# One transposition per head in the 256-key blocks, and the last group's queries transposed straight from the projection's pairs

## The chip, the core and the metric

The kernel runs on one core of a Trainium2 chip. The metric is device time in microseconds (us), the median of three runs; lower is better. The engines by their names in the profile: PE is TensorE (PEld its weight loads), DVE is VectorE, ACT is ScalarE, POOL is GpSimd, SP is SyncE, which computes nothing and issues DMAs (a line with SPq is one such issue).

## The reference

`x` is [1024, 512]. It is normalized by rows, goes through causal attention and through a feed-forward block whose weights are 4-bit integers, and the second gates the first:

```python
def attn(x, Wq, Wk, Wv, Wo, q_norm_w, k_norm_w):   # 32 heads, 8 groups of keys and values, head 128
    q, k, v = (x @ Wq.T), (x @ Wk.T), (x @ Wv.T)   # split into heads
    q, k = rmsnorm(q, q_norm_w), rmsnorm(k, k_norm_w)
    scores = einsum('bkgqd,bksd->bkgqs', qg, k) / sqrt(128)
    bias = where(rel > 0, -1e30, slopes * rel)     # causal, with a slope per head
    out = einsum('bkgqs,bksd->bkgqd', softmax(scores + bias), v)
    return out @ Wo.T

xn = layernorm(x)
s = attn(xn)
g = silu((silu(xn @ gate) * (xn @ up)) @ down)     # gate, up, down: (int - zero) * scale, 1792 wide
return x + s * g
```

## The kernel before

**Precision.** Every product is made in 16-bit halves. A float32 operand is split into a high half and a low half in fp16, and a product is three matmuls (high x high, high x low, low x high; `mm3`, L107 to L111). So "a split" is a copy to the high half (mostly on ScalarE) and a subtraction for the low half (on VectorE or GpSimd). The two halves lie side by side in one tile, so that one DMA can transpose both.

**Phases.** The feed-forward block comes first (0 to about 218 us). Then come twelve projections (to about 491 us): for each pair of groups one of keys and values (`kv`) and two of queries (`q`), each of eight tiles of 128 rows. The steps of attention start inside the last two projections, one at every second tile, and fill the rest of the time.

**A projection** (`class Projection`, from L484). `norms` (L509) sums the squares of the raw weights over the partitions by a matmul with ones; its PSUM tile comes from `spare` (L481). `tile` (L560) makes one row tile by 12 matmuls into a PSUM bank; banks come in turn from the tags "m" and "o", with two buffers each, and ScalarE copies the result into `f` and sums the squares of each head. After each four tiles `queue_half` (L754) sets due steps for what follows: `inverse` and `newton` (the inverse root), `normalize` on GpSimd (L622, L626), `halves` on VectorE (L628: a copy and a subtraction, giving the pair `a16`), `transposed` (L642: a DMA transposition of the pair into `tr`, L644) and `store` (L647: `tr` to DRAM). The last projection, that of group 7's queries, is treated apart: its eight tiles are spread over the attention steps, one pair of tiles in each fourth block. `wo_factors` (L794) prepares a scale for each group's rows of the output weight, with one matmul of its own (L801).

**Attention.** Work is cut into units (group, block of 256 queries, head), four units to a block, and each unit into two query tiles of 128 rows; one query tile is one step. A block of queries `qb` looks at the first (qb+1) x 256 keys, so the blocks are named by their keys here: 256, 512, 768 or 1024. The order of the blocks in a group is `FIRST_ORDER` for group 0 (1024, 768, 512, 256), `ORDER` for groups 1 to 6 (768, 1024, 256, 512) and `LAST_ORDER` for group 7 (768, 1024, 512, 256) (L45 to L47). `step(n)` (L960) is a software pipeline written out by hand. In step n:

- `scores` (L834) for query tile n, in PSUM tag "s" of two 2-bank buffers;
- `exponentials` (L845) for tile n-1: VectorE adds the bias and takes the row's minimum (L854, in the profile DVE row and pf), ScalarE makes the exponentials and their sum (L855);
- `split_hi` (L858) for n-3, on ScalarE (L865), and `split_lo` (L867) for n-4, on VectorE (L874), which ends with the DMA transposition of the probabilities, `pT<-p` (L875), issued by SP;
- `values` (L879) for n-9 (`AV_LAG`): the matmuls `av` of the transposed probabilities with the values;
- `heads_hi` and `heads_lo` for n-10, which split the heads' outputs, and `out_proj` (L910) and `accumulate` (L935) for the block before.

```python
        for stage, lag in ((exponentials, 1), (split_hi, NQT + 1), (split_lo, NQT + 2)):
            if at(n - lag):
                stage(*at(n - lag))
```

In the 256-key block the first query tile has 128 keys, the second 256: their pairs of halves are 256 and 512 columns wide (2 and 4 column blocks of 128).

**What else a step carries.** In the second head of a block SP loads the next block's queries from DRAM (`load_queries`, L788, `qT<-qd`). In the fourth head of the third block of a group `relative` (L822; `trel`, 1024 columns, on GpSimd, L830) and `load_keys` for the next group are done, and in the fourth head of the fourth block `load_values`. The output weight's rows are loaded, scaled (L813) and split (L819, L820, the tile `wol`) by `load_wo`, `scale_wo` and `split_wo` over eight steps in each group. In group 7 `gate_load` fetches the gate and x for each block, 1 MB each.

**Queues.** All DMAs are issued by SP, in the order of the program, and an issue that waits holds back those behind it. The same holds for each engine's instructions. The program's order is the order in which the functions above are called.

Of the kernel before, what the change touches and what calls it, by code (L numbers as in the profile page):

```python
# [21 lines left out]
P = 128  # L22
# [3 lines left out]
HKV = 8  # L26
# [18 lines left out]
FIRST_ORDER = (3, 2, 1, 0)  # L45
ORDER = (2, 3, 0, 1)
LAST_ORDER = (2, 3, 1, 0)  # L47
# [3 lines left out]
FINISH_BLOCK = 3  # L51
KEYS_BLOCK = 2
VALUES_BLOCK = 3
# [5 lines left out]
GATE_LOADS = [25, 26, 28, 30]  # L59
GATE_SUMS = [27, 28, 30, 31]  # L60
GATE_STEP = 2
PF_BUFS = 5
P16_BUFS = 5

# [7 lines left out]
def attention_gated_by_ffn_kernel(ctx, tc, x, gu_w, gu_z, gu_s, dn_w, dn_z, dn_s, wq, wkv, wo, qnw, knw, out):  # L72
# [408 lines left out]
    def spare(k, name):  # L481
        return ps2(name)[:, 0, :] if k else pair(name)[:, 0, :]

    class Projection:  # L484
# [24 lines left out]
        def norms(self):  # L509

            n = self.n
            pn = spare(self.k, f"n2_ps{self.k}")
            te.matmul(pn[:, 256 : 256 + n], lhsT=ones_bf, rhs=self.sb[:, :n], start=True, stop=True)
            if self.kind == "kv":
                for j in range(KT):
                    te.matmul(pn[:, :256], lhsT=ones_bf, rhs=self.sq[:, j, :], start=j == 0, stop=j == KT - 1)
            self.am = wp.tile([P, NH], F32, tag="am", name=f"am_{self.name}", bufs=2)[:, :n]
            ve.tensor_scalar(self.am, pn[:, 256 : 256 + n], 1.0 / W_SCALE**2, 1e-30, ALU.mult, ALU.max)
            rsqrt_seed(self.am, self.am)
            self.eps = eps[:, self.k, :n]  # L520
            ve.scalar_tensor_tensor(self.eps, self.am, 1e-6 * X_SCALE**2, self.am, ALU.mult, ALU.mult)
            if self.kind == "q":
                ve.tensor_tensor(self.eps, self.eps, steep, ALU.mult)
            if self.kind == "kv":
                self.al = wp.tile([P, 256], F32, tag="al", name=f"al{self.i}")
                ve.tensor_scalar(self.al, pn[:, :256], DM * (X_SCALE / V_SCALE) ** 2, 1e-30, ALU.mult, ALU.max)
                rsqrt_seed(self.al, self.al)
# [100 lines left out]
        def halves(self, t):  # L628
            f = self.f[t // HT][:, t % HT]
            n = self.n  # L630
            if self.kind == "q":
                a16 = fq.tile([P, 2, n, HD], F16, tag="a16", name=f"q16_{self.i}_{t}", bufs=5)
                hi, lo = a16[:, 0], a16[:, 1]
            else:
                a16 = fq.tile([P, 2, 2, HD], F16, tag="a16", name=f"k16_{self.i}_{t}", bufs=5)
                hi, lo = a16[:, :, 0, :], a16[:, :, 1, :]
                ve.tensor_tensor(f, f, wn.unsqueeze(1).to_broadcast([P, 2, HD]), ALU.mult)
            ve.tensor_copy(hi, f)
            ve.tensor_tensor(lo, f, hi, ALU.subtract)
            defer(2 if self.k == len(projections) - 1 else 1, lambda: self.transposed(t, a16))  # L640

        def transposed(self, t, a16):  # L642
            tr = fq.tile([P, 2 * self.n, P], F16, tag="tr", name=f"tr_{self.name}_{t}", bufs=5)
            sp.dma_start_transpose(tr, a16.rearrange("p a g d -> p (a g d)"))  # L644
            defer(4 if self.k == len(projections) - 1 else 2, lambda: self.store(t, tr))
# [108 lines left out]
    def queue_half(p, half):  # L754

        last = p is projections[-1]

        def due(steps, i, f):
            t = half * HT + i
            c = TILES - early + BS * (NB * (1 + t // 2) + FINISH_BLOCK) + 4 * (t % 2) if last else clock[0] + i  # L760
            finishing.setdefault(c + steps, []).append(f)

        due(0, 0, lambda: p.inverse(half))
        if p.by_root:
            due(1, 0, lambda: p.newton(half, True))
        else:
            for i in range(3):
                due((i + 1) // 2, 0, lambda i=i: p.newton(half, i == 0))
        for i in range(HT):
            t = half * HT + i  # L770
            due(4, i, lambda t=t: p.halves(t))
            due(2, i, lambda t=t: p.normalize(t))

    NB = S // QB
    blocks = [(g, qb) for g in range(HKV) for qb in (FIRST_ORDER if g == 0 else ORDER if g < HKV - 1 else LAST_ORDER)]
    units = [(g, qb, hh) for g, qb in blocks for hh in range(NH)]
# [11 lines left out]
    def load_queries(g, qb):  # L788
        qT[g, qb] = ap1.tile([P, NQT, 2, NH, P], F16, tag="qT", name=f"qT{g}_{qb}")
        sp.dma_start(  # L790
            qT[g, qb].rearrange("p t a g q -> p t (a g q)"), qd[g][qb * NQT : (qb + 1) * NQT].rearrange("t p c -> p t c")
        )

    def wo_factors(k):  # L794

        if k == 0:
            ve.tensor_tensor(rvs, rv, rv, ALU.mult)
            ve.tensor_tensor(swo16, rvs, swo, ALU.mult)
        elif k == 1:
            wo_ps.append(ps2("wo_ps")[:, 0, :HKV])  # L800
            te.matmul(wo_ps[0], lhsT=ones_bf, rhs=swo16, start=True, stop=True)  # L801
        else:
            ve.tensor_scalar(sg, wo_ps.pop(), 1.0 / W_SCALE**2, 1e-30, ALU.mult, ALU.max)
            rsqrt_seed(sg, sg)
            ve.reciprocal(isg, sg)
            ve.tensor_tensor(rvs, rv, sg, ALU.mult)
# [51 lines left out]
    def split_hi(u, qt):  # L858
# [5 lines left out]
        p16[u, qt] = ap1.tile([P, NT, 2, P], F16, tag="p16", name=f"p16_{u}_{qt}", bufs=P16_BUFS)[:, :nk]  # L864
        se.activation(p16[u, qt][:, :, 0, :], pf[u, qt], AF.Copy, scale=scale[:, qt : qt + 1])  # L865

    def split_lo(u, qt):  # L867
# [6 lines left out]
        ve.scalar_tensor_tensor(lo, p, scale, hi, ALU.mult, ALU.subtract)  # L874
        sp.dma_start_transpose(  # L875
# [22 lines left out]
    def heads_hi(u):  # L898
        oh = late[0].tile([P, QB], F16, tag="oh", name=f"oh{u}", bufs=8)
        ol = late[0].tile([P, QB], F16, tag="ol", name=f"ol{u}", bufs=8)  # L900
        se.activation(oh, av_ps[u], AF.Copy, scale=1.0 / P_SCALE)  # L901
        oT[u] = (oh, ol)

    def heads_lo(u):
        oh, ol = oT[u]
        ve.scalar_tensor_tensor(ol, av_ps.pop(u), 1.0 / P_SCALE, oh, ALU.mult, ALU.subtract)

    nb = len(units) // NH

    def out_proj(b, i, part):  # L910
        if part == 0:
            op_ps[b, i] = last_ps[i] if b == nb - 1 else ps1("m", f"op{b}_{i}")
        oh, ol = oT[b * NH + part]
        g = blocks[b][0]
        cols = slice(i * P, i * P + P)
        mm3(op_ps[b, i], (oh[:, cols], ol[:, cols]), (woh[g, part], wol[g, part]), part == 0, part == NH - 1)
# [3 lines left out]
    def gate_load(b):  # L920
        g, qb = blocks[b]
# [4 lines left out]
        gates[b] = gx  # L926

    def gate_partial(b, i):

        g, qb = blocks[b]  # L930
        gx, yt = gates[b], y_[0][:, qb * NQT + i, :]
# [3 lines left out]
    def accumulate(b, i):  # L935
        g, qb = blocks[b]
        ps = op_ps.pop((b, i))
# [7 lines left out]
        else:  # L945
            gt = gates[b][:, 0, i]
            ve.scalar_tensor_tensor(gt, ps, undo, gt, ALU.mult, ALU.mult)
            (ge if (b, i) == (nb - 2, NQT - 1) else ve).tensor_tensor(gt, gt, yt, ALU.add)
# [3 lines left out]
    nn, BS = len(order), NH * NQT  # L952
    late, y_ = [], []
# [6 lines left out]
    def step(n):  # L960
        nonlocal last_ps
        if n < nn:
            u, qt = order[n]
            g, qb, hh = units[u]
            b = u // NH
            if qt == 0 and hh == 1 and b + 1 < nb:
                load_queries(*blocks[b + 1])
            if qt == 0 and hh == 3 and g + 1 < HKV:
                if b % NB == KEYS_BLOCK:
                    relative(g + 1)  # L970
                    load_keys(g + 1)
                elif b % NB == VALUES_BLOCK:
# [11 lines left out]
        b, r = divmod(n - AV_LAG - BS - 2, BS)  # L984
        if 0 <= b < nb - 1 and r % NH == NH - 1 and n < nn + AV_LAG + 1:
            accumulate(b, r // NH)
        finish_step()
        m = n - AV_LAG - BS - 1

        def project():  # L990
            b, r = divmod(m, BS)
            if 0 <= b < nb - 1:
                out_proj(b, *divmod(r, NH))
# [5 lines left out]
        if done is not None and done // NH == nb - 1:  # L999
            if done % NH == 0:  # L1000
                last_ps = [ps2(f"op_last{i}")[:, 0, :] for i in range(NQT)]
            for i in range(NQT):
                out_proj(nb - 1, i, done % NH)
            if done % NH == NH - 1:
                accumulate(nb - 2, NQT - 1)
                for i in range(NQT):
                    accumulate(nb - 1, i)
        b, r = divmod(n - AV_LAG, BS)
        if r == 2 and b in GATE_LOADS:
            gate_load(nb - NB + GATE_LOADS.index(b))  # L1010
        if b in GATE_SUMS and 0 <= r - GATE_STEP < NQT:
            gate_partial(nb - NB + GATE_SUMS.index(b), r - GATE_STEP)
        for lead, act in ((WO_SPLIT, split_wo), (WO_SCALE, scale_wo), (WO_LOAD, load_wo)):
            w, r = divmod(m + lead, NB * BS)
            if 0 <= w < HKV and r in range(0, 2 * NH, 2):
                act(w, r // 2)

    last_ps, wo_ps = None, []
    relative(0)
    last_kv = len(projections) - 3  # L1020
    WO_FACTORS = [(last_kv, 5), (last_kv, 7), (last_kv + 1, 0)]
    early = 0
    for k, p in enumerate(projections):
        if k == len(projections) - 3:
            load_keys(0)
            load_values(0)
            load_queries(*blocks[0])
        for t in range(NT):
# [7 lines left out]
            if (k, t) in WO_FACTORS:  # L1036
                wo_factors(WO_FACTORS.index((k, t)))
            p.tile(t)
            finish_step()
            if t % HT == HT - 1:  # L1040
                queue_half(p, t // HT)
# [49 lines left out]
```

## Time and profile before

| | |
|---|---|
| median of three runs | 1071.33 us (1070.93 to 1071.74) |
| the profiled execution | 1077.16 us, span 1075.4 us |
| busy, share of the span | PE 94%, PEld 55%, DVE 82%, ACT 75%, POOL 38% |
| DMA queue of SP | 450,014 packets, 205.3 MB, 86.0% of 16 engines' time |
| idle of PE before `av`, for `pT<-p` | 26.1 us |
| idle of ACT before the high halves (L865), for `pT<-p` | 25.3 us |

The page cuts the span into 40 slices of 26.9 us each. A digit is the busy share of an engine in tenths, in the row PEclk the clock that TensorE was granted in tenths of full speed, and in the row DMA the mean busy share of the core's 16 DMA engines. Slices 0 to 7 are the feed-forward block, 8 to 17 the projections, and attention runs from slice 18 on. An idle time is put down to what ended it ("<- DMA pT<-p": the landing of a transposed tile of probabilities).

### The profile page before, as it was taken

The page shows a single profiled execution, that of the slowest core. Times are in us where ns is not written, and L with a number is a line of the kernel's source. Part 1 is how long each engine was busy: PE and PEld are TensorE (multiplying, and loading weights), DVE is VectorE, ACT ScalarE, POOL GpSimd, SP SyncE. Part 2 cuts the span into 40 slices and gives each one's busy share as a digit, 9 for nine tenths or more (in the row PEclk, how much of TensorE's full clock was granted, in tenths as well). Part 3 has the DMA queues.
Part 4 walks back from the last instruction along what each step waited for, and adds up shares of the span by engine and source line. Part 5 has one row for each costly group of instructions (what it writes and reads, how often), then busy time and mean ns, then how long its engine had stood idle before and what let it go on. Part 6 is the DMA issues. An engine that isn't in the chain of part 4 may idle for free.

```text
span 1075.4 us, 18459 instructions
## 1 busy us (share of the span) xinstructions
PE 1012.7 (94%) x5913; PEld 588.1 (55%) x5913; DVE 884.4 (82%) x1745; ACT 803.0 (75%) x2160; POOL 409.0 (38%) x375
## 2 busy tenths in 40 slices
PE   7899899999999999898899999999999899999996
PEld 4444377844444444345556566566565566665663
DVE  7888996638778787787789899798998797979985
ACT  5777645878778687688779688786896787978872
POOL 1688753124536446361404306016033050150542
PEclk8999999999999999999999999999999999999998
DMA  5133269446989989999989999899998999999995
GB/s 200 32 115 109 79 172 300 159 138 164 224 229 183 239 205 254 257 174 222 213 172 214 185 221 218 181 230 186 205 213 184 188 210 185 209 237 208 239 202 127
DMA packets 450111, 206.49 MB, mean 192 GB/s; under 512 B 394530, under 2 KB 404062, under 8 KB 450014
## 3 DMA queue, kind: packets, MB, share of 16 engines
q1 hardware_dynamic: 450014, 205.32, 86.0%
q8 instruction: 46, 0.75, 0.3%
q14 instruction: 51, 0.42, 0.1%
HBM read 79.42 MB, written 29.36 MB: 101 GB/s over the span
## 4 chain that ended last, share of the span: by engine, by line
PE 50%; DVE 13%; ACT 13%; DMA 12%; issue 8%; POOL 2%; SPq 1%; DVEq 0%; ACTq 0%; POOLq 0%
DMA pT<-p 7%; PE gu_ps L262 6%; PE av L109 3%; PE s L109 3%; PE s L111 3%; PE s L110 3%; PE av L111 3%; PE av L110 3%; PE op L111 3%; PE op L110 3%; PE op L109 3%; ACT pf L855 3%; ACT p L865 3%; DVE pf L854 2%; PE ps_q L109 2%
## 5 line engine op out<-in xcount | busy, mean ns | idle before, releaser
L874 DVE SCALAR_TENSOR_TENSOR p<-pf,row,p 128x1024 f16<-128x1024 f32 (+7 forms) x256 | 221.1, 864 | 36.1 <-ACT p L865 33.4
L855 ACT ACTIVATE pf<-pf,row 128x1024 f32<-128x1024 f32 (+7 forms) x256 | 197.3, 771 | 46.7 <-DVE row L854 44.2
L854 DVE CUSTOM_DVE_ANT_0 pf<-s,trel,cs 128x1024 f32<-128x1024 f32 (+7 forms) x256 | 207.3, 810 | 16.7 <-PE s L111 15.5
L865 ACT ACTIVATE p<-pf,row 128x1024 f16<-128x1024 f32 (+7 forms) x256 | 196.7, 769 | 29.5 <-DMA pT<-p 25.3
L109 PE MATMUL av<-pT,vT 128*128 128x256 f16 (+1 forms) x640 | 169.4, 265 | 26.3 <-DMA pT<-p 26.1
L813 POOL TENSOR_SCALAR wor<-wor,rvs 128x512 f32<-128x512 f32 x32 | 53.0, 1656 | 313.0 <-DMA wor<-in_wo 313.0
L110 PE MATMUL av<-pT,vT 128*128 128x256 f16 (+1 forms) x640 | 169.4, 265 | 0.0
L111 PE MATMUL av<-pT,vT 128*128 128x256 f16 (+1 forms) x640 | 169.2, 265 | 0.0
L109 PE MATMUL s<-kT,qT 128*128 128x512 f16 (+3 forms) x384 | 126.1, 328 | 4.2 <-DVE row L854 4.1
L110 PE MATMUL s<-kT,qT 128*128 128x512 f16 (+3 forms) x384 | 126.2, 329 | 0.0
L111 PE MATMUL s<-kT,qT 128*128 128x512 f16 (+3 forms) x384 | 124.6, 328 | 0.0
L109 PEld LDWEIGHTS <-vT 128*128 128x128 f16 x640 | 63.2, 99 | 71.5 <-issue 17.3
L109 PE MATMUL ps_q<-wh_q,xth 128*128 128x512 f16 x256 | 97.8, 382 | 0.3 <-ACT wh_q L551 0.3
L110 PE MATMUL ps_q<-wl_q,xth 128*128 128x512 f16 x256 | 97.7, 381 | 0.4 <-DVE wl_q L552 0.4
L111 PE MATMUL ps_q<-wh_q,xtl 128*128 128x512 f16 x256 | 97.5, 381 | 0.0
L110 PE MATMUL op<-wol,oh 128*128 128x512 f16 x248 | 94.5, 381 | 1.0 <-POOL wol L820 1.0
L111 PE MATMUL op<-woh,ol 128*128 128x512 f16 x248 | 94.7, 382 | 0.0
L109 PE MATMUL op<-woh,oh 128*128 128x512 f16 x248 | 94.4, 381 | 0.0
L110 PEld LDWEIGHTS <-vT 128*128 128x128 f16 x640 | 63.2, 99 | 40.6 <-issue 2.7
L901 ACT ACTIVATE oh<-av 128x256 f16<-128x256 f32 x128 | 47.9, 374 | 42.8 <-PE av L111 41.6
L626 POOL TENSOR_TENSOR f_q<-f_q,inv_q 128x512 f32<-128x512 f32 x64 | 77.0, 1229 | 1.3
L820 POOL TENSOR_TENSOR wol<-wor,woh 128x512 f16<-128x512 f32 x32 | 50.2, 1570 | 66.4 <-ACT woh L819 66.4
(193 smaller groups left out, 2267.8 us busy)
## 6 DMA issues: line engine op xcount, KB each, us to landing
qd<-tr_q SPq DMA_DIRECT2D x64, 256.0 KB, 3.7
qT<-qd SPq DMA_DIRECT2D x32, 512.0 KB, 4.5
wq<-in_wq SPq DMA_DIRECT2D x32, 256.0 KB, 4.0
wo_sq<-in_wo SPq DMA_DIRECT2D x8, 1024.0 KB, 9.0
wor<-in_wo SPq DMA_DIRECT2D x32, 256.0 KB, 3.6
gui<-in_gu_w SPq DMA_DIRECT2D x13, 512.0 KB, 3.7
wkv<-in_wkv SPq DMA_DIRECT2D x16, 256.0 KB, 3.8
vd<-v SPq DMA_DIRECT2D x8, 512.0 KB, 4.3
```

The source lines that it names most:

```text
L109: te.matmul(ps, lhsT=lh, rhs=rh, start=first, stop=False)
L110: te.matmul(ps, lhsT=lh, rhs=rl, start=False, stop=False)
L111: te.matmul(ps, lhsT=ll, rhs=rh, start=False, stop=last)
L262: te.matmul(banks[j][:, k, :], lhsT=w[:, j, ws], rhs=x[:, j, k * 512 : k * 512 + 512], start=x is xth, stop=x is xtl)
L626: ge.tensor_tensor(f, f, ib, ALU.mult)
L813: ge.tensor_scalar(wor[g, i], wor[g, i], rvs[:, g : g + 1], None, ALU.mult)
L820: ge.tensor_tensor(wol[g, i], raw, woh[g, i], ALU.subtract)
L854: ve.tensor_tensor_reduce(p, ps, trel[g][:, S - w :], cs[:, hh : hh + 1], 3e38, ALU.add, ALU.min, least[:, c])
L855: se.activation(p, p, AF.Exp, bias=least[:, c], scale=-1.0, accum_out=total[:, c])
L865: se.activation(p16[u, qt][:, :, 0, :], pf[u, qt], AF.Copy, scale=scale[:, qt : qt + 1])
L874: ve.scalar_tensor_tensor(lo, p, scale, hi, ALU.mult, ALU.subtract)
L901: se.activation(oh, av_ps[u], AF.Copy, scale=1.0 / P_SCALE)
```

## The change

1. In the 256-key blocks both query tiles of a head share one tile of pairs, laid out as (key tile, half, query tile, key). The quarter that the mask leaves out, the second key tile of the first query tile, is set to zero by GpSimd. One DMA transposition of eight column blocks per head takes the place of one of two and one of four; it is issued after the second tile's low half.
2. The last projection's pairs are kept, in five buffers, and each is transposed straight into the queries' tile `qT` of group 7, at a fixed step (`LAST_QUERIES`). The transposition into `tr`, the store to DRAM and the load from it fall away for this group. The steps of the pairs are given one by one (`LAST_PAIRS`), as are those of the inverse roots (`LAST_ROOTS`). The last projection makes its rows 512 to 1023 first.
3. `relative` and `load_keys` go from step 22 of a group to step 4 of it, `load_values` from step 30 to step 24.
4. `norms` takes its PSUM tile from tag "m" in place of "s". The matmul of `wo_factors` joins that of the last projection's `norms`, in the same tile.
5. The schedule is written as tables (`q_at`, `op_at`, `acc_at`, `GATE_LOADS`, `GATE_SUMS`) that name the same steps as before for `load_queries`, `out_proj`, `accumulate` and the gate.

```diff
+KEYS_STEP = 4
+VALUES_STEP = 24
+LAST_ROOTS = {1: 24, 0: 36}
+LAST_PAIRS = {4: 46, 5: 78, 6: 110, 7: 142, 2: 174, 3: 221, 0: 224, 1: 229}
+LAST_QUERIES = {4: 217, 5: 219, 6: 225, 7: 227, 2: 233, 3: 235, 0: 241, 1: 243}
...
     def spare(k, name):
-        return ps2(name)[:, 0, :] if k else pair(name)[:, 0, :]
+        return ps1("m", name) if k else pair(name)[:, 0, :]
...
+            wo = pn[:, 384 : 384 + HKV]
+            if self.k == len(projections) - 1:
+                te.matmul(wo, lhsT=ones_bf, rhs=swo16, start=True, stop=True)
...
+            if self.k == len(projections) - 1:
+                wo_factors(wo)
...
-            defer(2 if self.k == len(projections) - 1 else 1, lambda: self.transposed(t, a16))
+            if self.k == len(projections) - 1:
+                last_pairs[t] = a16
+            else:
+                defer(1, lambda: self.transposed(t, a16))
...
         def due(steps, i, f):
-            t = half * HT + i
-            c = TILES - early + BS * (NB * (1 + t // 2) + FINISH_BLOCK) + 4 * (t % 2) if last else clock[0] + i
+            if last and i is None:
+                c = TILES + LAST_ROOTS[half]
+            elif last:
+                c = TILES + LAST_PAIRS[half * HT + i] - 4
+            else:
+                c = clock[0] + (i or 0)
             finishing.setdefault(c + steps, []).append(f)
...
+    def last_queries(t):
+        g, qb = HKV - 1, t // NQT
+        if (g, qb) not in qT:
+            qT[g, qb] = ap1.tile([P, NQT, 2, NH, P], F16, tag="qT", name=f"qT{g}_{qb}", bufs=2)
+        sp.dma_start_transpose(
+            qT[g, qb][:, t % NQT].rearrange("p a g q -> p (a g) q"), last_pairs.pop(t).rearrange("p a g d -> p (a g d)")
+        )
...
-        p16[u, qt] = ap1.tile([P, NT, 2, P], F16, tag="p16", name=f"p16_{u}_{qt}", bufs=P16_BUFS)[:, :nk]
+        if units[u][1]:
+            p16[u, qt] = ap1.tile([P, NT, 2, P], F16, tag="p16", name=f"p16_{u}_{qt}", bufs=P16_BUFS)[:, :nk]
+        elif qt == 0:
+
+            both = ap1.tile([P, NT, 2, P], F16, tag="p16", name=f"p16_{u}", bufs=P16_BUFS)
+            both = both.rearrange("p t a k -> p (t a k)")[:, : 4 * NQT * P].rearrange("p (t a i k) -> p t a i k", t=2, a=2, i=NQT)
+            ge.memset(both[:, 1, :, 0, :], 0.0)
+            for i in range(NQT):
+                p16[u, i] = both[:, : i + 1, :, i, :]
+            p16[u] = both
...
+        if u in p16:
+            if qt == NQT - 1:
+                sp.dma_start_transpose(
+                    pT[u][:, :NQT].rearrange("p t a (i q) -> p (t a i) q", i=NQT),
+                    p16.pop(u).rearrange("p t a i k -> p (t a i k)"),
+                )
+            return
...
-                if b % NB == KEYS_BLOCK:
+                if n % (NB * BS) == KEYS_STEP:
                     relative(g + 1)
                     load_keys(g + 1)
-                elif b % NB == VALUES_BLOCK:
+                elif n % (NB * BS) == VALUES_STEP:
                     load_values(g + 1)
...
-            if (k, t) in WO_FACTORS:
-                wo_factors(WO_FACTORS.index((k, t)))
-            p.tile(t)
+            if (k, t) == (len(projections) - 3, HT + 1):
+                wo_squares_sums()
+
+            row = t if k < len(projections) - 1 else (t + HT) % NT
+            p.tile(row)
             finish_step()
             if t % HT == HT - 1:
-                queue_half(p, t // HT)
+                queue_half(p, row // HT)
```

## The prediction

> **What bounds the kernel now.** I read, in this order: the page's slices, what TensorE waited for, the DMA queue's timeline, TensorE's timeline at one wait, and windows cut at the blocks. The profiled execution took 1077.16 us with a span of 1075.4; the median of the runs shown is 1071.33, so the sums below are made against 1077.16 and scaled by 1071.33 / 1077.16 = 0.9946.
>
> ```profile
> PE   7899899999999999898899999999999899999996
> PEclk8999999999999999999999999999999999999998
> DMA  5133269446989989999989999899998999999995
> ```
> TensorE is the bound from end to end (94% busy), and from slice 18 on, where attention runs, the DMA engines are as full. What TensorE still loses there stands in its list of waits (us in total, times, longest):
>
> ```profile
> PE av L109 <- DMA pT<-p: 26.1, 21, 3.2
> PE s L109 <- DVE row L854: 4.1, 6, 1.7
> PE wo_ps L801 <- DVE swo L798: 2.6, 1, 2.6
> ```
> So 26 us go to probabilities that are not yet transposed. Why they are late is seen in SP's queue, here over the blocks of 256 and 512 keys of group 4:
>
> ```profile
> 818.98 2.14 SPq L875 DMA_TRANSPOSE pT<-p  x1
> 821.17 1.30 SPq L644 DMA_TRANSPOSE tr_q<-q  x1
> 822.57 3.83 SPq L875 DMA_TRANSPOSE pT<-p  x3
> 826.49 0.53 SPq L790 DMA_DIRECT2D qT<-qd  x1
> 827.12 1.17 SPq L875 DMA_TRANSPOSE pT<-p  x1
> 828.38 0.53 SPq L649 DMA_DIRECT2D qd<-tr_q  x1
> 828.97 1.24 SPq L644 DMA_TRANSPOSE tr_q<-q  x1
> 830.25 5.00 SPq L875 DMA_TRANSPOSE pT<-p  x3
> ```
> Start and length: one issue follows the other without a gap. By the view of line 875 an issue lasts at least 1167 ns however small the tile (median 1428, 3813 at most). VectorE had finished a low half at 838.77 that SP issued only at 844.62, 5.9 us late. SP is the bound of these two blocks. In the blocks of 768 keys the same lateness is back to 0.03 us, in those of 1024 it grows to 2 or 3 us, because there the DMA engines are full (share 1.14).
>
> A wait of over 2 us costs twice (start, length of one, idle before it):
>
> ```profile
> 843.86 0.28 PE L109 MATMUL av<-pT,vT 128*128 128x256 f16 x1 [2.18 <-DMA pT<-p]
> 845.68 0.63 PE L109 MATMUL s<-kT,qT 128*128 128x512 f16 x1
> 848.42 0.38 PE L111 MATMUL op<-woh,ol 128*128 128x512 f16 x1
> ```
> The 512-column matmul goes from 0.38 to 0.63 us for about 3.4 us, and the window over 836.4 to 858.1 has a granted clock of 0.92 of 1.00: (1 - 0.92) x 21.7 = 1.7 us lost again. [...]
>
> **The change, part by part.**
>
> 1. *One transposition per head in the 256-key blocks.* It removes 32 issues of 1.17 to 1.24 us (two of 2 and 4 column blocks become one of 8). An 8-block transposition has rows: the queries' and those of 512 keys, 1.23 to 1.25 us when SP is not held back. SP saves about 8 x 1.2 - 4 x 1.25 = 4.6 us per group, in the block where it falls behind. The queries of the last group also leave groups 1 to 4: two issues of 1.3 and two of 0.53 us each, 3.7 us per group. The lateness at the end of a 1024-key block (2 to 3 us) is then gone within the next block, and the 512-key block after it (8 x 1.25 + 0.56 us of queries, about 11.5 us with the gaps) fits its 13 to 14 us. So the waits for tiles of 256 and 512 keys go. Counting the av matmuls (values run 9 steps behind scores), they are, from group 1 to the start of group 7: 0.56, 0.75, 0.35, 1.41, 1.91, 0.30, 2.18, 2.29, together 9.75 us, and 1.7 us of half clock. Six waits end with a 1024-key tile and stay: 1.36, 2.30, 0.97, 1.25, 0.26, 1.59. Six in group 0 stay (6.5 us). The last, 2.15 at 1055.2, is the first tile of the last block behind 1 MB of gate loads; one issue less brings it forward by 1.2 us, its doubled size takes back some 0.6: -0.7 (between 0 and -3.9 with the half clock after it).
> 2. *The queries' way, middle groups.* TensorE's waits of 0.88 (593), 1.01 (742, for POOL's wol) and 1.07 (744) stand next to that projection's small POOL and VectorE steps, which move away: -2.1, taking the two larger.
> 3. *What lands elsewhere.* Each halves pair is 0.42 + 0.69 = 1.11 us of VectorE. Five go to step 14 of the 1024-key blocks, where VectorE is 21.1 of 22.3 us busy: at most 5 x 1.11 = 5.5, at least 0, since SP is later than VectorE there and the next block has slack (14.8 of 17.8). I take +1.5. Three go to steps 221, 224 and 229, into blocks where VectorE sets the pace (13.1 of 13.6): between 0 and 3.3, I take +2.3.
> 4. *Last group's transpositions.* 8 x 1.25 - 4 x 0.56 = +7.8 us of SP in steps 217 to 243. Two fall into the 1024-key block, where SP lies 5.2 us behind at its end: +1.9 us, straight onto the wait of 1.59 at 1036.8, and perhaps past the 2 us that bring the half clock. Between 0 and 3.6, I take +2.0. Each also waits for its pair, and the transpositions of probabilities queue behind it; the pairs are there (halves 4 steps or more ahead).
> 5. *Keys and values earlier.* Keys (0.58 us of SP, 512 KB) move from the 256-key to the 768-key block, where lateness is nil: 0, or 0.6 per group if that cover goes. The 2.94 us of POOL for trel move with them. In the old place VectorE's low half took 1.98 to 2.21 instead of 1.28 us where it met trel and wol. In the new place VectorE has less slack (16.9 of 19.1): between -3 and +5 for seven groups, I take +1.
> 6. *The norms in the m banks.* During the projections tiles take turns in m and o, two banks each. A ninth tenant per projection makes norms wait for tile 6 and tile 2 for tile 0. ScalarE copies late there: tile 0 of projection 4 (from 0) is copied from 308.78 to 310.38, tile 2 started at 307.07, so it would start 3.4 us later. But TensorE runs 4 tiles ahead of ScalarE there and gives the time back at later waits (2.1 us and a half clock at 393 and 0.8 at 370, both for ScalarE, shrink). The wait for swo (2.56, and 1.7 of half clock) goes, yet norms then wait for tile 6, evacuated at 440.6, and tile 2 for tile 0 at 445.1 where it started at 445.86. From below -4.3, from above +4; I take +0.3.
> 7. *Zeroing on POOL.* No row of that shape: between 0.2 us (a 128x128 memset) and 1.65 (wol, 128x512) each. POOL is idle at steps 19 to 25 and only SP waits for it: 0. Without that cover at most 1.65 per head.
>
> Sum: -9.75 - 1.7 - 0.7 - 2.1 + 1.5 + 2.3 + 2.0 + 1.0 + 0.3 = -7.1. 1077.16 - 7.1 = 1070.1, times 0.9946 = **1064.3 us**.
>
> [...]
>
> **Rivals.**
>
> *Slower: the last group's queries come late.* For the chain speaks that SP was 5.9 us behind in the same block of group 4. A query tile issued that late, with 1.24 us to issue and 5.0 to land (2.1 to 7.1 in its view), needs 12.1 us against 5 steps of some 1.65 = 8.2: TensorE waits 3.9 for scores, plus 1.7 at half clock, 5.6 per pair of tiles. For three of the four pairs 16.8. Without part 4 the sum is -9.1; -9.1 + 16.8 = +7.7, or 1078.9 us. It decides from a lateness of about 2 us (8.2 - 1.24 - 5.0) at step 217. Against it: the 256-key block just before now clears the backlog.
>
> *No change: VectorE takes over.* In the 512-key blocks it is 12.4 to 13.1 us busy of 13.6 to 14.2, and in the 768-key blocks 15.6 of 16.1. If half of the 13.5 us (9.75 + 1.7 + 2.1) comes back as waits for row, -7.1 becomes -0.4: 1070.9. Against it: such waits are 4.1 us in all now.
>
> *Larger gain.* Also gone: the 2.30 at 672.9 with its half clock (4.0), the rest of the last wait (3.2) and the swo stall in full (4.3 + 0.3). -7.1 - 11.8 = -18.9: 1052.5.
>
> That the change would not do what it says is out: SP's order has 44 DMA instructions fewer, 32 transpositions, 8 stores and 4 loads.
>
> **How the numbers follow.** Forecast 0.55 (own range 1058 to 1069), larger gain 0.13, no change 0.13, slower 0.19. Within 0.2% (2.1 us, about what a measurement can tell) means 1069.2 to 1073.5. Faster 0.68, same 0.13, slower 0.19. The range reaches to 1054, next to the larger gain, and to 1075, into the slower case; some 0.05 is left out below and 0.12 above.
>
> **What would show it.** Part 1: the total of av's waits for pT falls from 26 to between 13 and 17 us, and the half clock after 843 is gone. Part 4: a wait of over 3 us near the end of the last 1024-key block, or waits of s for qT from step 224 on. Part 6: waits of n_ps and ps_q for ScalarE in the projections. Wrong is the forecast if waits for row grow by more than 5 us, or if the last group takes over 4 us longer.

## The result, and the profile after

The changed kernel takes **1066.42 us** (median of seven runs, 1065.24 to 1068.11) against 1070.93 us for the kernel before beside it: ratio 0.9958, 95% interval 0.9944 to 0.9971, so 3.1 to 6.0 us faster. The forecast was 1064.3 us, in a range of 1054 to 1075. The profiled execution took 1066.42 us, just the median, with a span of 1064.6 us.

The slices of the changed kernel, to be read against those of before:

```profile
PE   7899899999989999898799999999999999999986
PEclk9999999999999999999999999999999999999998
DMA  6123259447988989989999999899999998999995
```
Little moves at this scale: TensorE stays the bound (94% again) and the DMA engines stay full (SP's queue takes 85.4% of 16 engines' time, 86.0% before). The list of what TensorE waited for (us in total, times, longest) shows more:

```profile
PE av L114 <- DMA pT<-p: 15.5, 14, 2.7
PE s L114 <- DVE row L878: 12.1, 19, 1.8
PE n_ps L518 <- DVE v L595: 5.6, 3, 2.7
```
The waits of `av` for transposed probabilities fall from 26.1 to 15.5 us. But the waits of the scores for VectorE's `row` rise from 4.1 to 12.1 us: of 10.6 us gained, 8.0 are lost again. The wait of the single matmul `wo_ps` (2.6) is gone; waits of the norms take its place, as the forecast's part 6 had it (the last one ends at 440.07 us and lasts 2.71), but they are waits for VectorE, where the forecast named ScalarE.

SP's queue in the blocks of 256 and 512 keys of group 4 (start, length), the stretch that was issued without a gap before:

```profile
806.68 2.66 SPq L910 DMA_TRANSPOSE pT<-p  x2
809.40 0.57 SPq L803 DMA_DIRECT2D vT<-vd  x1
811.92 1.23 SPq L910 DMA_TRANSPOSE pT<-p  x1
813.20 0.60 SPq L807 DMA_DIRECT2D qT<-qd  x1
816.19 1.23 SPq L910 DMA_TRANSPOSE pT<-p  x1
817.87 9.38 SPq L915 DMA_TRANSPOSE pT<-p  x6
```
Now there are gaps: 809.97 to 811.92 and 813.80 to 816.19 us. SP waits for the probabilities, no longer the other way round.

To see where the time went I cut every profile at the first exponentials of a group. The columns are the start of the projections, from there to the first exponential, group 0, groups 1 to 5, groups 6 and 7, the span (us):

```
                 start  proj.  group 0  1 to 5  6 and 7   span   median ratio to before
before           218.3  234.2    97.4   361.1   164.4   1075.4
changed          217.0  234.8    96.1   347.5   169.2   1064.6   0.9958 [0.9944, 0.9971]
changed_again    218.4  235.4    96.6   347.1   169.3   1066.7   0.9953 [0.9936, 0.9970]
merge_only       215.8  233.9    96.8   350.2   164.4   1061.1   0.9935 [0.9913, 0.9957]
merge_again      216.8  234.6    97.4   352.3   164.6   1065.5   0.9934 [0.9910, 0.9957]
sp_pad           216.3  233.9    97.0   353.2   164.6   1065.1   0.9940 [0.9917, 0.9963]
no_merge         217.8  235.7    96.5   349.3   172.2   1071.6   1.0005 [0.9987, 1.0024]
keys_22          217.1  234.3    96.2   348.3   169.1   1065.1   0.9962 [0.9942, 0.9981]
norms_s          219.5  234.4    96.2   348.8   171.8   1070.6   0.9946 [0.9926, 0.9966]
pairs_22         217.6  235.5    96.7   343.6   168.7   1062.1   0.9931 [0.9906, 0.9956]
via_dram         217.1  235.5    96.9   352.5   164.4   1066.5   0.9944 [0.9923, 0.9964]
pairs_early      215.9  235.3    95.8   346.1   166.4   1059.4   0.9926 [0.9907, 0.9945]
queries_early    217.3  234.9    96.7   347.4   168.1   1064.5   0.9932 [0.9906, 0.9959]
pairs_spread     217.7  235.2    96.2   346.4   167.4   1062.8   0.9921 [0.9894, 0.9948]
```
The last column is worked out from the times, the others from one profile each. The change gains 13.6 us in groups 1 to 5 and loses 4.8 in groups 6 and 7. Many single blocks come out alike to 0.1 us from profile to profile, so the middle columns tell more than the medians, whose intervals are some 3 to 6 us wide. They have their own noise: the same kernel profiled twice differs in groups 1 to 5 by 0.4 us (347.5 and 347.1) or 2.1 (350.2 and 352.3), and a stretch of 3.4 us in which TensorE gets half its clock (granted clock 0.50) costs up to 1.7 us and comes after some waits and not after others as long (last section). Before has two such stretches in groups 1 to 5, the changed kernel none, so up to 3.4 of the 13.6 us are theirs.

### The profile page after: what moved, and what is told of

Same layout as the page of the kernel before. It is cut to its first block, busy times and chain, and to the rows that moved or that the text cites. A ratio compares the mean times of both kernels' runs of the same rounds, so it can differ in the third digit from the quotient of the medians.

```text
span 1064.6 us, 18405 instructions
## 1 busy us (share of the span) xinstructions
PE 1002.7 (94%) x5913; PEld 584.6 (55%) x5913; DVE 886.1 (83%) x1745; ACT 802.7 (75%) x2160; POOL 413.9 (39%) x407
## 3 DMA queue, kind: packets, MB, share of 16 engines
q1 hardware_dynamic: 454942, 203.21, 85.4%
## 4 chain that ended last, share of the span: by engine, by line
PE 48%; DVE 17%; ACT 13%; issue 10%; DMA 8%; SPq 2%; POOL 2%; DVEq 0%; ACTq 0%; POOLq 0%
PE gu_ps L267 6%; DMA pT<-p 4%; PE s L114 4%; DVE pf L878 3%; PE s L116 3%; PE s L115 3%; PE op L114 3%; PE op L115 3%; PE av L114 3%; PE op L116 3%; PE av L116 3%; PE av L115 3%; ACT p L898 2%; ACT pf L879 2%; PE ps_q L114 2%
## 5 line engine op out<-in xcount | busy, mean ns | idle before, releaser
L907 DVE SCALAR_TENSOR_TENSOR p<-pf,row,p 128x1024 f16<-128x1024 f32 (+7 forms) x256 | 227.8, 890 | 23.5 <-ACT p L898 20.3
L114 PE MATMUL av<-pT,vT 128*128 128x256 f16 (+1 forms) x640 | 167.8, 262 | 15.5 <-DMA pT<-p 15.5
L114 PE MATMUL s<-kT,qT 128*128 128x512 f16 (+3 forms) x384 | 125.0, 325 | 12.4 <-DVE row L878 12.1
L115 PE MATMUL op<-wol,oh 128*128 128x512 f16 x248 | 94.3, 380 | 0.0
```

The costliest lines, as they stand in the source:

```text
L114: te.matmul(ps, lhsT=lh, rhs=rh, start=first, stop=False)
L115: te.matmul(ps, lhsT=lh, rhs=rl, start=False, stop=False)
```

## The experiments

The second table that the readings rest on is SP's lateness: from the end of VectorE's low half to the start of SP's issue of its transposition, mean over groups 1 to 5, worked out from the traces (us).

```
                 768 keys  1024 keys  256 keys  512 keys
before             0.74      1.28       3.15      3.00
merge_only         0.64      0.74       1.13      1.85
merge_again        0.78      1.22       1.18      1.61
sp_pad             0.65      0.89       1.84      2.03
no_merge           0.35      0.46       2.30      0.45
via_dram           1.35      1.67       1.37      1.53
changed            0.41      0.54       0.65      0.14
```

### merge_only and merge_again: part 1 alone, in the kernel before

```diff
...
+        if u in p16:
+            if qt == NQT - 1:
+                sp.dma_start_transpose(
+                    pT[u][:, :NQT].rearrange("p t a (i q) -> p (t a i) q", i=NQT),
+                    p16.pop(u).rearrange("p t a i k -> p (t a i k)"),
+                )
+            return
```


> The kernel before with part 1 of the change alone (one transposition per head in the 256-key blocks), everything else as before. Theory A (SP's issues bound the 256- and 512-key blocks, and merging frees 8 x 1.2 - 4 x 1.25 = 4.6 us of SP per group): TensorE's wait of av for pT falls from 26.1 to 16-20 us, and the time falls by 3 to 5 us, ratio to the kernel before 0.995 to 0.997. Rival B (it is the last group's queries leaving the middle groups, 3.7 us of SP in groups 1 to 4, that frees SP): the wait stays above 22 us, ratio 0.999 to 1.001.

Measured: ratio 0.9935, a gain of 7.0 us (4.6 to 9.3), more than expected and, by the medians, more than the whole change. The list of TensorE's waits:

```profile
PE av L109 <- DMA pT<-p: 17.5, 19, 2.8
PE s L109 <- DVE row L854: 5.1, 6, 1.7
```
The wait for `pT` falls by 8.6 us, and the wait for `row` hardly moves (4.1 to 5.1). Lateness in the 256-key blocks falls from 3.15 to 1.13 us with all of the last group's queries still in the queue. Rival B, by which the merge would do nothing, falls.

> The kernel before with the merge alone, once more beside the others on one chip. Theory A: ratio 0.992 to 0.995, av's wait 16 to 19 us, last two groups 164.4 us; with it, whether the rest of the change adds or takes: pairs_spread faster than this by 0.2 to 0.4% if the direct way gains once its pairs are hidden, no faster if it costs as much as it saves.

Measured: 0.9934, wait 19.9 us (16 to 19 expected), last two groups 164.6 us. The gain of the merge repeats; the second question is taken up with pairs_spread.

### no_merge: everything but part 1

```diff
-        if units[u][1]:
...
-        elif qt == 0:
...
+        p16[u, qt] = ap1.tile([P, NT, 2, P], F16, tag="p16", name=f"p16_{u}_{qt}", bufs=P16_BUFS)[:, :nk]
...
```


> The changed kernel with two transpositions per head in the 256-key blocks again, everything else as changed. Theory A: the wait of av for pT goes back from 15.5 to 20 us or more, mostly in blocks of 256 and 512 keys, the time rises by 2 to 5 us over the changed kernel, ratio 0.998 to 1.001. Rival B: the wait stays near 16 us, ratio 0.995 to 0.997.

Measured: 1.0005, no gain at all. The wait for `pT` rises only to 19.1 us, below what theory A said. Lateness in the 256-key blocks is back at 2.30 us. Yet groups 1 to 5 take 349.3 us, no more than with the merge alone (350.2 and 352.3): there the rest of the change, the queries' leaving in it, does as much as the merge alone, and both together (347.5) little more. What is lost stands in the projections (235.7 us) and in groups 6 and 7, which take 172.2 us. In these SP has five transpositions of probabilities in a row behind the last group's queries and 1 MB of gate loads, and TensorE, in its own timeline, the longest wait (start, length of one, idle before it):

```profile
960.82 1.31 SPq L817 DMA_TRANSPOSE qT<-q  x1
962.22 2.12 SPq L899 DMA_TRANSPOSE pT<-p  x1
964.39 0.58 SPq L946 DMA_DIRECT2D gx<-gd  x1
965.02 0.46 SPq L947 DMA_DIRECT2D gx<-in_x  x1
965.59 7.95 SPq L899 DMA_TRANSPOSE pT<-p  x5
973.64 1.26 SPq L817 DMA_TRANSPOSE qT<-q  x1
```
```profile
973.43 0.27 PE L114 MATMUL av<-pT,vT 128*128 128x256 f16 x1 [3.78 <-DMA pT<-p]
```
This is the forecast's slower rival, by another victim: what comes late are the probabilities behind the queries, not the queries. The changed kernel has no wait for `pT` of over 0.5 us at this place, the start of group 7, so the merge is what keeps it away, as the forecast said against that rival.

### sp_pad: the merge, with other issues in the place of those it saved

```diff
+        if u in p16 and qt == 0:
+            for i in range(2):
+                pad = dram.tile([1, NH], F32, name=f"pad{u}_{i}")
+                sp.dma_start(pad, cs[0:1])
```


> The kernel before with the merge alone, and two DMAs of 16 bytes from SP per head of the 256-key blocks, issued where the first of the two transpositions was: 8 x 0.5 = 4 us of SP per group, about what the merge freed, and no bytes to speak of. Theory A (the number of SP's issues is what the merge saves): the gain of the merge is lost, av's wait for pT goes from 17.5 back to 21-26 us, ratio to the kernel before 0.997 to 1.000. Rival L (the merge gains through its transfers, one landing for two, not through SP's time): ratio 0.992 to 0.995, wait near 17.5 us.

Measured: 0.9940, which lies in the range of rival L. But the expectation had the price of an issue wrong: such a DMA takes 0.25 us of SP (median of 64), not 0.5.

```profile
811.15 0.72 SPq L887 DMA_DIRECT2D pad<-cs  x2
812.03 1.24 SPq L890 DMA_TRANSPOSE pT<-p  x1
```
So the padding gave back about 2 us per group, under half of the 4.6. Lateness in the 256-key blocks rises from 1.13 and 1.18 to 1.84 us, a third of the way back to 3.15, in step with SP's time; the wait of `av` rises to 22.8 us, within theory A's numbers; the time, 1067.56 against 1066.45 us for the merge alone on the same chip, can't tell. That SP's time sets the lateness is supported; that it alone makes the whole gain was not shown.

### pairs_22: five pairs in the 256-key block

```diff
-LAST_PAIRS = {4: 46, 5: 78, 6: 110, 7: 142, 2: 174, 3: 221, 0: 224, 1: 229}
+LAST_PAIRS = {4: 54, 5: 86, 6: 118, 7: 150, 2: 182, 3: 221, 0: 224, 1: 229}
```


> The changed kernel with the pairs of tiles 4, 5, 6, 7 and 2 made at step 22 of groups 1 to 5 (in the 256-key block) and not at step 14 (in the 1024-key block). Theory C (a pair costs its full 1.11 us of VectorE in the 1024-key block, because VectorE sets the pace there): the two waits of s for row at steps 19 and 20 of groups 1 to 5 (0.38 and 0.59 us) go, 4.9 us in all, ratio 0.991 to 0.993. Rival D (the waits come from the keys' and trel's new place, or VectorE is as full in the 256-key block): the waits stay or move, ratio 0.995 to 0.997.

Measured: 0.9931, as theory C expected, though the interval overlaps that of the changed kernel. Total wait for `row` 6.8 us in place of 12.1; of the waits at steps 19 and 20 those of group 1 alone are left. Windows cut at the 1024-key and the 256-key block of group 4 (bounds, length, busy time and count on PE, PEld, DVE, ACT, POOL, then clock, DMA share, GB/s), the changed kernel first, then pairs_22:

```profile
772.60:796.30 23.70, 23.70 (x166) 15.36 (x165) 22.16 (x37) 20.43 (x36) 9.88 (x7) 1.00 1.10 217
796.30:812.80 16.50, 15.51 (x124) 11.02 (x122) 12.47 (x35) 10.74 (x35) 5.49 (x7) 1.00 1.02 197
```
```profile
772.30:794.50 22.20, 22.20 (x153) 14.19 (x152) 20.64 (x35) 20.25 (x37) 8.45 (x6) 1.00 1.07 227
794.50:811.20 16.70, 16.44 (x135) 12.09 (x134) 13.51 (x37) 10.68 (x34) 7.10 (x8) 1.00 1.13 197
```
With the pair, the exponentials take 23.70 us through the 1024-key block, without it 22.20: VectorE is busy 1.52 us longer (22.16 against 20.64; the pair itself is 1.11 of it), and the block is 1.50 us longer: nothing hides the pair there. In the 256-key block it is 13.51 of 16.70 us and adds 0.2. TensorE pays a block later, in the changed kernel's timeline at 800.55 and 803.26 us:

```profile
800.55 0.22 PE L114 MATMUL s<-kT,qT 128*128 128x128 f16 x1 [0.36 <-DVE row L878]
803.26 0.27 PE L114 MATMUL s<-kT,qT 128*128 128x256 f16 x1 [0.59 <-DVE row L878]
```
Groups 1 to 5 take 343.6 us against 347.5 and 347.1: 3.5 to 3.9 us.

### keys_22: keys, `trel` and values at their old steps

```diff
-KEYS_STEP = 4
-VALUES_STEP = 24
+KEYS_STEP = 22
+VALUES_STEP = 30
```


> The changed kernel with keys and trel at step 22 and values at step 30 of a group, as before. Theory E (trel at step 4 costs only in group 0, where it stands on GpSimd ahead of the projections' normalizations): the waits of s for row between 485 and 505 us fall from 4.7 to 2 us or less, other groups change little, ratio 0.992 to 0.994. Rival F (the old place costs more, since trel slows VectorE's low halves there, 1.98 to 2.21 against 1.28 us): ratio 0.997 to 0.999, with waits of av or s in the 256-key blocks of every group.

Measured: 0.9962, neither theory's number and the same as the changed kernel. The cause that theory E names is there: the waits of `s` for `row` between 485 and 505 us fall from 4.7 to 2.4 us (2 or less expected), and in the changed kernel's timeline of GpSimd `trel` takes 3.73 us ahead of the projection's inverse roots and normalizations,

```profile
470.77 3.73 POOL L854 TENSOR_SCALAR trel<-trel 128x1024 f32<-128x1024 f32 x1
474.47 0.22 POOL L627 TENSOR_TENSOR nwt_q<-ms_q,inv_q 128x16 f32<-128x16 f32 x1
```
and the first block takes 45.0 us by its exponentials against 42.7 in keys_22. But group 0 as a whole takes 96.1 and 96.2 us; that the probabilities of the next block set its end either way is my reading and was not tested. Over all groups the move costs nothing that can be measured.

### norms_s: the norms in tag s again

```diff
-        return ps1("m", name) if k else pair(name)[:, 0, :]
+        return ps2(name)[:, 0, :] if k else pair(name)[:, 0, :]
```


> The changed kernel with the norms' PSUM tile in tag s again, everything else as changed. The forecast gave that step +0.3 us (between -4.3 and +4). Theory M (the step costs: the norms of the last projection wait 2.7 to 3.9 us for a bank that VectorE reads, and tiles wait at 306 us): from the first projection's first matmul to the first exponential 233 to 234 us against 234.8 and 235.4, ratio 0.992 to 0.995. Rival N (the waits come back as waits for ScalarE): the same within 0.5 us, ratio 0.995 to 0.997.

Measured: 0.9946, and 234.4 us for the projections against 234.8 and 235.4. The two theories are not told apart. The profiles put the cost of the move at 0.4 to 1.0 us, but both profiles of the changed kernel have a stretch of half clock in the projections (granted clock 0.99 over them in both) and norms_s has none there (1.00). The two runs with the norms in tag "m" and no such stretch, keys_22 and via_dram (mean granted clock of the whole execution 0.994 in both), take 234.3 and 235.5 us, so the cost lies somewhere between nothing and 1 us. The wait of the norms only changes its releaser:

```profile
PE n_ps L518 <- ACT sb_q L510: 3.7, 3, 2.4
```

### via_dram, pairs_early, queries_early, pairs_spread: the last group's queries

via_dram takes only the direct way back, with the pairs at the steps of before:

```diff
-                last_pairs[t] = a16
+                defer(2, lambda: self.transposed(t, a16))
...
-                if due[0] < HKV - 1:
-                    load_queries(*due)
+                load_queries(*due)
...
```


> The changed kernel with the last group's queries on their way through DRAM again (pairs at the steps of the kernel before, transposed and stored there, loaded by block), everything else as changed. Theory J (the direct way costs the last two groups more than it saves in groups 1 to 4 once the merge has freed SP): the last two groups take 164 to 165 us against 169.2, groups 1 to 5 348 to 351 against 347.5, ratio 0.991 to 0.994, at or below the changed kernel. Rival K (the queries leaving is needed to clear the lateness): groups 1 to 5 take over 353 us, ratio over 0.997.

Measured: 0.9944 (0.991 to 0.994 expected), groups 6 and 7 in 164.4 us as expected, groups 1 to 5 in 352.5, above theory J's numbers and below rival K's.

pairs_early keeps the direct way, but with eight buffers, so that the pairs are made at the same old steps:

```diff
-LAST_PAIRS = {4: 46, 5: 78, 6: 110, 7: 142, 2: 174, 3: 221, 0: 224, 1: 229}
+LAST_PAIRS = {4: 54, 5: 58, 6: 86, 7: 90, 2: 116, 3: 120, 0: 148, 1: 152}
-                a16 = fq.tile([P, 2, n, HD], F16, tag="a16", name=f"q16_{self.i}_{t}", bufs=5)
+                a16 = fq.tile([P, 2, n, HD], F16, tag="a16", name=f"q16_{self.i}_{t}", bufs=8)
```


> The changed kernel with eight buffers for the pairs in place of five, and all eight made where the kernel before made them (steps 54, 58, 86, 90, 116, 120, 148, 152, in 256-key blocks); the last group's transpositions stay where they are. Theory C: groups 1 to 5 as with the pairs at step 22 (343 to 345 us against 347.5 of the changed kernel), and the three pairs at steps 221, 224 and 229 cost no more, 1.5 to 2.5 us in the last two groups (169.2 before); ratio 0.989 to 0.992. Rival D (VectorE's work only moves): ratio 0.994 to 0.997.

Measured: 0.9926, just outside theory C's numbers; groups 1 to 5 in 346.1 us (343 to 345 expected), groups 6 and 7 in 166.4. Against the changed kernel the latter is 2.8 us less, against pairs_22, which has the three late pairs too but no half clock after 1044 us (the changed kernel has 0.50 there for 3.4 us), 2.3: that is the price of the three pairs at steps 221, 224 and 229. Against via_dram it is 2.0 us more, the price of the eight transpositions themselves; and in groups 1 to 5 the direct way takes 346.1 against 352.5 us (via_dram, at a mean granted clock of 0.994 against 0.996, has one stretch of half clock there).

queries_early adds to pairs_early four buffers for the queries' tiles and earlier steps:

```diff
-LAST_QUERIES = {4: 217, 5: 219, 6: 225, 7: 227, 2: 233, 3: 235, 0: 241, 1: 243}
+LAST_QUERIES = {4: 211, 5: 213, 6: 217, 7: 219, 2: 225, 3: 227, 0: 229, 1: 231}
...
```


> As the run with all pairs early, and four buffers for the queries' tiles, so that the last group's eight transpositions are issued at steps 211, 213, 217, 219, 225, 227, 229 and 231, none in the 1024-key block of the last group. Theory H (the last group's extra time is SP's: transpositions of 1.2 to 1.8 us ahead of the probabilities where SP is already late): the last two groups take 1.5 to 3 us less than with the pairs early alone, ratio 0.987 to 0.990. Rival I (the DMA engines are full and the bytes cost the same wherever they are issued): no difference within 1 us.

Measured: 0.9932, groups 6 and 7 in 168.1 us, 1.7 us more than pairs_early (it has half clock after 1044 us, pairs_early hasn't; mean granted clocks 0.994 and 0.996). Theory H falls: the two waits at the end of the 1024-key block (1.66 and 1.46 us in pairs_early) go, and others come up earlier (2.79 us at 949.8, 1.78 at 970.2). These eight issues cost no less at these steps; other places were not tried.

pairs_spread takes one pair per 256-key block, again with eight buffers:

```diff
+LAST_PAIRS = {4: 30, 5: 54, 6: 86, 7: 118, 2: 150, 3: 182, 0: 186, 1: 214}
...
```


> The changed kernel with eight buffers for the pairs and one pair per 256-key block (steps 30, 54, 86, 118, 150, 182, 186, 214). Theory C: one pair at a time is hidden there, as with the five pairs at step 22: groups 1 to 5 take 344 to 345 us (343.6 with five pairs, 346.1 with all eight two by two, 347.5 changed), the last two groups 166 to 167 (169.2 changed); ratio 0.989 to 0.992, the fastest so far. Rival: 0.993 or more, if the gains don't add.

Measured: 0.9921, the lowest ratio of all; 1064.64 us against 1066.45 for the merge alone beside it, and the intervals overlap. Groups 1 to 5 take 346.4 us where 344 to 345 were expected, groups 6 and 7 167.4 (166 to 167). It is faster than the kernel before; that it beats the merge alone, or the changed kernel, the runs don't settle.

### changed_again: which waits bring the half clock

> The changed kernel once more, so that the variants stand beside it on the same chip, and a second profile tells which of its waits and half-clock stretches come back. [...]

Measured: 0.9953. The waits come back. Half clock follows those at 440 and 1044 us again, and the one at 512 us, where the changed kernel's profile had none. That wait, in the changed kernel's timeline and then in this run's:

```profile
512.47 0.28 PE L114 MATMUL av<-pT,vT 128*128 128x256 f16 x1 [2.57 <-DMA pT<-p]
512.58 0.27 PE L115 MATMUL av<-pT,vT 128*128 128x256 f16 x1
```
```profile
514.76 0.39 PE L114 MATMUL av<-pT,vT 128*128 128x256 f16 x1 [3.04 <-DMA pT<-p]
514.95 0.42 PE L115 MATMUL av<-pT,vT 128*128 128x256 f16 x1
515.16 0.42 PE L116 MATMUL av<-pT,vT 128*128 128x256 f16 x1
```
The matmuls after it start 0.11 us apart in the one, at a granted clock of 1.00 from 512.5 to 517.9 us, and 0.21 in the other, at 0.61 from 514.8 to 518.2. Some waits differ by over 0.3 us (2.57 and 3.04, 2.71 and 3.90), and the two profiles don't show whether it is the length of a wait that decides.

## Why the prediction was right, point by point

The time, the sign and the range came out, and the likeliest case was the right one. That a gain of 7.0 us was forecast and 4.5 measured is in part luck: two errors of opposite sign stand behind it. On the profiled executions the gain was 10.7 us where the sum had 7.1, 3.6 too little; from there to the medians it shrinks by 6.2 us, where the scaling took off 0.1. One of the forecast's own signs of being wrong was passed: waits for `row` grew by 8.0 us, more than the 5 it named. The other was not: the last group takes 97.4 us against 94.3, 3.1 longer and not 4.

- **Part 1 (-12.15).** Right in place, and the mechanism is supported: `av`'s wait for `pT` fell to 15.5 us (13 to 17 expected), the waits of 2.18 and 1.91 us in the short blocks and the half clock after 843 are gone. The merge alone gains 10 to 14 us of span against that one profile of before, but 7.0 us by the medians. The part joins two reliefs of SP that overlap: the queries' leaving (no_merge, with the rest of the change) brings groups 1 to 5 to 349.3 us, the merge to 350.2 and 352.3, both to 347.5.
- **The scaling by 0.9946 failed.** It spread the 5.8 us by which the profiled execution of before lay above its median evenly over the span. Much of them is likely half clock. That execution has seven stretches of it between 390 and 1060 us, the changed kernel's has two; at 3.4 us each with a granted clock of 0.50, so up to 1.7 us lost, that is up to 8.5 of the 10.7 us between the two. Two of the seven (from 499.9 and 513.5 us) follow waits that the changed kernel has too, with a granted clock of 1.00 after them (1.70 and 3.16 us in before, 1.82 and 2.57 in the changed kernel), so it was not the going of the waits that took these two away. The mean granted clocks of the two profiled executions:

```profile
core 0: 1075.4 us, clock 0.983
core 0: 1064.6 us, clock 0.993
```
The first is as low as the lowest of the 81 other executions of this kernel whose clock is on record (median 0.990); the second is about usual (median of seven 0.992). So the gain on the profile (7.1 forecast, 10.7 measured) is larger than by medians (4.5). The sum also counted the 1.7 us of half clock after 843 as certain; in the profiles of the two kernels seven of ten waits of over 2 us came with one (last section).
- **Part 2 (-2.1)** can't be set against one number, since the forecast counted SP's relief by the same queries in part 1. With the merge in place the direct way as a whole saves about 6 us in groups 1 to 5 by one profile each (352.5 against 346.1, of which up to 1.7 is one stretch of half clock).
- **Part 3, first term (+1.5), failed.** Nothing hides a pair in the 1024-key block: five cost 3.5 to 3.9 us more there than in the 256-key block. I had both ends (0 and 5.5) and chose near the lower, on the ground that SP was later than VectorE there. That cover was not there, and it is not the merge that took it away: no_merge, without the merge, has the same 23.7 us in the 1024-key blocks of groups 2 to 5, and a block later the same waits, here in group 3:

```profile
736.88 0.27 PE L114 MATMUL s<-kT,qT 128*128 128x256 f16 x1 [0.59 <-DVE row L878]
```
Whether the queries' leaving took the cover, or there never was any, was not tested. The second term (+2.3) measured 2.3 to 2.8.
- **Part 4 (+2.0)** measured 2.0. It isn't bound to the 1024-key block, though: moved out of it (queries_early), the cost stays.
- **Part 5 (+1.0)** measured nothing beyond the noise; **part 6 (+0.3)** between nothing and 1.0 us in the projections, and its new waits are for VectorE, not for ScalarE; **part 7 (0)** holds, with 0.31 us for each zeroing.
- **The rivals.** "VectorE takes over" came half true: its mark, waits for `row` up by more than 5 us, was passed (8.0). But pairs_22 brings them down to 6.8 us with the same work on VectorE, so it is the place of five pairs, not VectorE's load as a whole. The slower rival's mechanism, with the probabilities late in place of the queries, appears as soon as the merge is taken out (no_merge). The larger gain didn't come: the wait of 2.30 us at 672.9 became one of 1.05, the last wait went from 2.15 to 2.66 and 2.22 in two profiles, and the norms' wait replaced that for swo.

What stays open: whether parts 2 to 6 together cost anything. The merge alone is at 0.9935 and 0.9934, the whole change at 0.9958 and 0.9953, and the intervals overlap.

## What to carry to other kernels

Where many small DMAs leave from one queue, measure how late the queue issues after its data is ready, block by block; one issue instead of two was worth 0.65% here, though it moved more bytes (207.4 MB against 205.3 in the whole kernel). Before work is moved into a block, see how full its engine is there: in group 4 a pair of 1.11 us lengthened a block that VectorE fills to 93% by 1.50 us, and one that it fills to 76% by 0.2. And before a sum is made against one profiled execution, compare it with the median and look where its excess lies.

## What the runs showed of the hardware

**Half clock comes with some waits and not with others as long.** In the profiles of the two kernels every stretch of half clock between 390 and 1060 us has a granted clock of 0.50 for 3.4 us, so it costs up to 1.7 us. The profile of before has seven, from 394.1, 435.0, 499.9, 513.5, 674.0, 844.6 and 1056.3 us, that of the changed kernel two, from 439.4 and 1043.6. From the projections on TensorE has ten waits of over 2 us in the two. Seven come with such a stretch: 2.15, 2.18, 2.30, 2.56 and 3.16 us in before, 2.66 and 2.71 in the changed kernel; it starts between 0.7 us before the end of the wait and 1.1 us after it. Three don't: 2.29 us (to 981.9) in before, 2.57 (to 512.5) and 2.32 (to 518.6) in the changed kernel, all with a clock of 1.00 after them. The other two stretches of before follow shorter waits, of 1.32 us (to 392.8) and 1.70 (to 497.6), while one of 1.91 us (to 833.9) has none. So the 2 us that the forecast went by are no limit here: five of the six longer waits of before cost twice, and one didn't. The length of a wait alone does not tell whether half clock comes; what else decides was not shown.

**An issue has no fixed price.** On SP a 16-byte store took 0.25 us (median in sp_pad), and in before the queries' 256 KB stores and 512 KB loads 0.51 and 0.56 (medians), the transpositions of probabilities 1.17 us and up; my padding was mis-sized because I took the second for the first.
